# A graph attention layer on one core: 88 instead of 64 edge groups taken out of the gather

## The chip, the cores and the metric

The kernel runs on one core of a Trainium2 chip. The metric is device microseconds (us) of one execution. Engines are named as in the profile: PE (matmul), DVE (vector), ACT (scalar), POOL (GpSimd), SP (sync, which here only issues DMAs).

## The reference

One layer of graph attention, with a residual and a normalisation, over N = 12500 nodes and E = 400000 edges of 64 features each:

```python
h_src, h_dst = x[src], x[dst]
e = leaky_relu(concat([h_src, h_dst, edge]) @ W_attn + b_attn, 0.01)
m = concat([h_src, edge]) @ W_ne
alpha = softmax of e over the edges of the same dst
z = segment_sum(alpha * m, dst)
out = layernorm(x + relu(concat([x, z]) @ W_out))
```

The edges come sorted by `dst`. `dst` is drawn as 12500 u² with u uniform, so low nodes have many edges and high nodes few.

## The kernel before, in words

All work of interest is in `sorted_path` (line 53). Edges stand in 782 groups of 512: 128 partitions by T = 4 columns. The kernel treats two kinds of group differently.

**Gathered groups.** Groups 64 to 781 fetch the rows of their sources from a table in device memory. `gather` (L273) issues on POOL, for each group, four indirect DMAs of 128 rows (L280) into a tile `zx`. Four groups share a tile, and the pool holds ZB = 8 tiles. The 718 groups form 46 batches: 43 of 16 groups and, from `ENDS`, batches of 12, 12 and 6. A batch has four tiles, so the eight buffers are two batches deep: the gather of tile i of batch k+2 can begin when the products of tile i of batch k are done with its buffer. Per tile, `scores` (L305) computes the edge part of the score on DVE (L314, L316), adds the gathered part (L321, the first instruction that needs the gather), makes a one-hot of the destination (L323) and picks the destination's part (L328, L331). Per batch, `softmax` (L562) runs a segmented softmax as a chain that goes back and forth between DVE, PE and ACT: segmented scans on DVE, then L497 and L500 on PE turn a column into a line and back (`to_line`, `to_col`), and DVE waits for that at L604 and L633. Then `weights` (L669) scales the one-hots and `products` (L684, the matmuls at L689) sums weighted rows into PSUM; `add_in` (L696, L706) adds that into an SBUF ring of accumulators. Products of tiles 0 and 1 come at once, those of tiles 2 and 3 in pieces during the softmax of the next batch (`some_products`). Output blocks of 128 nodes are finished four at a time by `finish0` to `finish3` (L878 to L947) when their edges are all in.

**Dense groups.** Groups 0 to 63 belong to the lowest nodes and are not gathered. Each passes three stations:

- A *look* finds the source's part of the score: `look_products` (L376, L380) multiplies a one-hot of the source's position in its block by the scores of all 98 blocks, and `look_scores` (L383) picks the right block on DVE (L392 to L395), adds the edge's part (L389, L390) and the destination's part (L397 to L400). Two looks are done per batch, in batches 1 to 32.
- A softmax of their own, in four rounds of 16 groups, runs at batches 8, 16, 24 and 32, in the tile phase and beside the ordinary one. Such a batch is called resting here.
- A *count*: `dense_counts` (L403) builds, for each of the four columns, the position one-hot times the softmax weight (L412 on DVE) and a one-hot of block and destination slot (L410, L411 on ACT), and multiplies them (L417 on PE). `dense_sum` (L420, L426) adds the result to the tile `counts`, which thus holds the summed weight of each source node for each of ND = 16 destination slots. Two counts per batch, in batches 10 to 41. `edge_products` (L446, L452) and `edge_sum` (L460) sum the edge features of the same groups.

When a *chunk* of groups has been counted, `node_products` (L462, 13 matmuls at L467) multiplies `counts` by all of x, `node_pick` (L471) and its followers put the sums into accumulators `accd` and `acce` for nodes 0 to 127, and `counts` is cleared (L479). There are ten chunks.

Everything stands in a written-out order (`manual_schedule`): each engine executes its instructions as the Python code issues them. Inside the softmax, the generator stops at five places and calls `dense_step(n)` there, which is where dense work is put into the waits of the chain.

Of the kernel before, what the change touches and what calls it, by code (L numbers as in the profile page):

```python
# [15 lines left out]
P = 128  # L16
T = 4
# [11 lines left out]
LOWS = 1  # L29
# [5 lines left out]
DB = 4  # L35
EACH = 2
CHUNKS = ((16, 1), (8, 3), (4, 6))
NODS = (2, 3, 4, 5)
ND = 16
HC = 8  # L40
NOD = max(NODS)
# [11 lines left out]
def sorted_path(ctx, tc, x, dst, idx, edge, w_ne, w_attn, b_attn, w_out, out, flag):  # L53
# [46 lines left out]
    assert HC * ND == P and HC * D <= 512 and sum(chunk_sizes) == DG and len(NODS) == DB  # L100

    def nodes_of(g):
        return NODS[g // BS]

# [29 lines left out]
    fars = const.tile([P, NK + DB + 1], F32, name="fars")  # L134
# [4 lines left out]
    both = const.tile([P, D], F32, name="both")  # L139

# [4 lines left out]
    places = const.tile([P, NB * NOD], F32, name="places")  # L145
# [61 lines left out]
    def dense_list(d):  # L207

        srcs = pre.tile([P, BS, 2 * T], I32, name="dense_srcs", bufs=DB)
        nc.sync.dma_start(out=srcs, in_=idx[d * BS:(d + 1) * BS].rearrange("g p c -> p g c"))  # L210
        return srcs

    def dense_places(d, srcs):

        at = slice(d * BS, (d + 1) * BS)
        parted = tiny.tile([P, T, BS], I32, name="parted")
# [166 lines left out]
    def look_scores(g, j, loads, found):  # L383

        ed, wrow = loads
        many = nodes_of(g)
        pr = feats.tile([P, SG, T, D], F32, name="pr", bufs=1)
        total = tiny.tile([P, 3, T], F32, name="total")
        nc.vector.tensor_tensor(pr[:, 0], ed[:, j], w_edge.to_broadcast([P, T, D]), op=OP.mult)  # L389
        nc.vector.tensor_reduce(total[:, 0], pr[:, 0], axis=AX.X, op=OP.add)  # L390
        hits = work.tile([P, T, NB], BF16, name="hits", bufs=1)
        nc.vector.tensor_tensor(hits, count_[:, 0:NB].unsqueeze(1).to_broadcast([P, T, NB]),  # L392
                                high[:, :, g:g + 1].to_broadcast([P, T, NB]), op=OP.is_equal)
        nc.vector.tensor_tensor(found, found, hits, op=OP.mult)
        nc.vector.tensor_reduce(total[:, 1], found, axis=AX.X, op=OP.add)  # L395
        at = pr[:, 1, :, 0:many]
        nc.vector.tensor_tensor(at, slots[:, 0:many].unsqueeze(1).to_broadcast([P, T, many]),  # L397
                                slot_[:, :, g:g + 1].to_broadcast([P, T, many]), op=OP.is_equal)
        nc.vector.tensor_tensor(at, at, wrow[:, j].unsqueeze(1).to_broadcast([P, T, many]), op=OP.mult)
        nc.vector.tensor_reduce(total[:, 2], at, axis=AX.X, op=OP.add)  # L400
        nc.vector.tensor_reduce(y_dense[:, :, g % BS], total.rearrange("p c t -> p t c"), axis=AX.X, op=OP.add)

    def dense_counts(g):  # L403

        lows = work.tile([P, T, P], F32, name="lows", bufs=LOWS)
        highs = []
        wide = NB * nodes_of(g)
        for t in range(T):
# [3 lines left out]
            nc.vector.tensor_scalar(lows[:, t, :], count_, low[:, t, g:g + 1], kept[:, t, g % (2 * BS):g % (2 * BS) + 1],  # L412
# [3 lines left out]
        for t in range(T):  # L416
            nc.tensor.matmul(to, lows[:, t, :], highs[t], start=(t == 0), stop=(t == T - 1))  # L417
# [10 lines left out]
    def dense_weights(g0, n):  # L428
# [4 lines left out]
        for j in range(n):  # L433
# [12 lines left out]
    def edge_products(g0, n, ep, w, bank_):  # L446

        assert n == 2 == EACH
        many = nodes_of(g0)
        z = bank_[:, T * NB:T * NB + n * many].rearrange("p (g n) -> p g n", n=many)  # L450
        for t in range(T):
            nc.tensor.matmul(z, ep[:, t], w[:, t], start=(t == 0), stop=(t == T - 1))  # L452
        return g0, n, z

    def edge_sum(g0, n, z):

        for g in range(n):
            of = slice(g * D, (g + 1) * D)
# [103 lines left out]
    def softmax(k, about, carry, d=None):  # L562

        G = sizes[k] if d is None else BS
# [8 lines left out]
        if k and G < BS:  # L573
# [7 lines left out]
        if d is not None:  # L581
            nc.scalar.activation(yraw[:, :, 0:BS], y_dense, AF.Copy)
# [72 lines left out]
        if meets:  # L655
# [9 lines left out]
            nc.vector.memset(rtm[:, R:R + 1], FLOOR)  # L665
# [1007 lines left out]
```

## Time and profile before

| what | us |
|---|---|
| median of 3 runs (lowest, highest) | 3665.47 (3664.61, 3672.32) |
| the profiled execution, its own time | 3668.67 |
| its span, first to last instruction | 3666.9 |
| busy: POOL | 2723.0 |
| busy: PE, DVE, ACT | 2016.1, 1982.1, 943.7 |
| mean granted clock of PE | 0.667 of full speed |

The profiled execution is 1.8 us longer than its span, and 3.2 us above the median. A group of instructions is a row `line engine operation out<-in xcount | busy us, mean ns of one | idle us before them <-what ended it`. A row of the timeline is `start, duration, engine, line, operation [idle before <-releaser]`.

### The profile page before, as it was taken

The page shows a single profiled execution, that of the slowest core. Times are in us where ns is not written, and L with a number is a line of the kernel's source. Part 1 is how long each engine was busy: PE and PEld are TensorE (multiplying, and loading weights), DVE is VectorE, ACT ScalarE, POOL GpSimd, SP SyncE. Part 2 cuts the span into 40 slices and gives each one's busy share as a digit, 9 for nine tenths or more (in the row PEclk, how much of TensorE's full clock was granted, in tenths as well). Part 3 has the DMA queues.
Part 4 walks back from the last instruction along what each step waited for, and adds up shares of the span by engine and source line. Part 5 has one row for each costly group of instructions (what it writes and reads, how often), then busy time and mean ns, then how long its engine had stood idle before and what let it go on. Part 6 is the DMA issues. An engine that isn't in the chain of part 4 may idle for free.

```text
span 3666.9 us, 32998 instructions
## 1 busy us (share of the span) xinstructions
PE 2016.1 (55%) x8505; PEld 1751.5 (48%) x8505; DVE 1982.1 (54%) x5065; ACT 943.7 (26%) x2202; POOL 2723.0 (74%) x2888
## 2 busy tenths in 40 slices
PE   0144443435555544756665576566657576665754
PEld 0144443334555544655554465555545455444554
DVE  5544444444554555556555565565556565545565
ACT  1211211212222222223322233232223233222221
POOL 6777777777777777777777777777777777777772
PEclk9999999997555555655565565556656565665555
DMA  9332332223333233333333333332323233322231
GB/s 123 71 65 62 66 70 59 59 60 68 66 64 80 57 72 63 70 67 67 70 77 64 69 65 68 66 82 58 75 47 83 54 65 70 65 59 60 55 67 24
DMA packets 488960, 242.90 MB, mean 66 GB/s; under 512 B 330131, under 2 KB 442810, under 8 KB 488762
## 3 DMA queue, kind: packets, MB, share of 16 engines
q1 hardware_dynamic: 393590, 144.58, 16.9%
q0 software_dynamic: 92128, 95.80, 15.6%
q8 instruction: 70, 1.15, 0.1%
q14 instruction: 128, 1.05, 0.1%
q10 hardware_dynamic: 3044, 0.33, 0.1%
HBM read 233.74 MB, written 6.73 MB: 66 GB/s over the span
## 4 chain that ended last, share of the span: by engine, by line
POOL 38%; PE 19%; issue 16%; DVE 14%; DMA 9%; ACT 3%; DVEq 1%; SPq 0%; POOLq 0%; ACTq 0%
POOL zx L280 38%; PE pg L689 13%; DMA zx<-table,srcs 8%; PE pg L417 2%; DVE acc L706 1%; DVE hot L323 1%; DVE pr L328 1%; DVE sdst L331 1%; PE pg L380 1%; PE lines L497 1%; DVE pr L314 1%; DVE level L636 1%; DVE fixed L316 1%; PE pg L918 1%; PE lines L500 1%
## 5 line engine op out<-in xcount | busy, mean ns | idle before, releaser
L280 POOL DMA_INDIRECT zx<-table,srcs x2808 | 2652.8, 945 | 855.8 <-issue 791.8
L689 PEld LDWEIGHTS pg<-w,zx 128*128 128x128 f32 x5600 | 1212.4, 332 | 76.9 <-issue 64.7
L689 PE MATMUL pg<-w,zx 128*128 128x24 f32 (+10 forms) x5600 | 1211.4, 391 | 57.6 <-issue 55.2
L497 PE MATMUL lines<-ident,bnd 128*1 128x128 f32 x200 | 60.5, 406 | 1193.1 <-ACT bnd L594 1178.9
L497 PEld LDWEIGHTS lines<-ident,bnd 128*1 128x1 f32 x200 | 14.8, 98 | 1218.0 <-ACT bnd L594 1202.2
L321 DVE TENSOR_TENSOR fixed<-fixed,zx 128x16 f32<-128x16 f32 (+3 forms) x184 | 33.9, 184 | 701.9 <-DMA zx<-table,srcs 698.4
L314 DVE TENSOR_TENSOR pr<-ze,fixed 128x1024 f32<-128x1024 f32 (+3 forms) x184 | 219.6, 1194 | 135.8 <-ACT fixed L311 133.8
L417 PE MATMUL pg<-big,lows 128*128 128x196 f32 (+3 forms) x512 | 257.2, 672 | 15.4 <-DVE lows L412 11.1
L316 DVE TENSOR_REDUCE fixed<-pr 128x16 f32<-128x1024 f32 (+3 forms) x184 | 221.1, 1202 | 6.3
L311 ACT ACTIVATE fixed<-wrow 128x144 f32<-128x144 f32 (+10 forms) x184 | 47.7, 259 | 595.6 <-issue 239.8
L312 ACT ACTIVATE zx<-ze 128x1024 f32<-128x1024 f32 (+3 forms) x184 | 191.0, 1038 | 8.6 <-DMA zx<-table,srcs 2.1
L589 ACT ACTIVATE soft<-turned 128x128 f32<-128x128 f32 x50 | 19.3, 386 | 664.8 <-DVE turned L587 664.8
L417 PEld LDWEIGHTS pg<-big,lows 128*128 128x128 f32 x512 | 146.0, 301 | 90.5 <-issue 71.9
L706 DVE TENSOR_TENSOR acc<-acc,pg 128x16 f32 (+10 forms) x718 | 132.1, 184 | 99.3 <-PE pg L689 33.0
L410 ACT ACTIVATE big<-places,place 128x196 f32<-128x196 f32 (+3 forms) x256 | 144.9, 566 | 0.0
L380 PE MATMUL pg<-s_src,big 128*128 128x98 f32 x512 | 136.9, 446 | 0.0
L467 PE MATMUL pg<-xall,counts 128*128 128x512 f32 (+1 forms) x260 | 129.5, 659 | 0.0
L411 ACT ACTIVATE big<-big 128x196 f32<-128x196 f32 (+3 forms) x256 | 125.3, 489 | 8.1
L380 PEld LDWEIGHTS pg<-s_src,big 128*128 128x128 f32 x512 | 125.6, 330 | 0.0
L323 DVE TENSOR_TENSOR hot<-fixed,drel 128x576 bf16<-128x576 f32 (+10 forms) x184 | 113.4, 616 | 6.4
L328 DVE TENSOR_TENSOR pr<-hot,fixed 128x576 f32<-128x576 bf16 (+10 forms) x184 | 112.6, 612 | 6.3
L331 DVE TENSOR_REDUCE sdst<-pr 128x16 f32<-128x256 f32 (+12 forms) x184 | 112.5, 611 | 6.4
(289 smaller groups left out, 2272.4 us busy)
## 6 DMA issues: line engine op xcount, KB each, us to landing
ze<-in_edge_dram SPq DMA_DIRECT2D x172, 512.0 KB
zx<-table,srcs POOLq DMA_INDIRECT x2808
ed<-in_edge_dram SPq DMA_DIRECT2D x32, 256.0 KB
low_of<-low_rows SPq DMA_DIRECT2D x64, 128.0 KB
ep<-in_edge_dram SPq DMA_DIRECT2D x64, 128.0 KB
table<-xall SPq DMA_DIRECT2D x7, 455.0 KB
ze<-in_edge_dram SPq DMA_DIRECT2D x8, 384.0 KB
out_dram<-yo SPq DMA_DIRECT2D x23, 128.0 KB
```

Of the source, the lines that this page charges most:

```text
L280: nc.gpsimd.indirect_dma_start(out=zx[0:r, g, t, 1:EW] if plain else zx[0:r, g, t, 0:EW], out_offset=None, in_=x[:, :] if plain else table ...
L312: nc.scalar.activation(zx[0:r, 0:n, :, EW:EW + D], ze[0:r, 0:n], AF.Copy)
L314: nc.vector.tensor_tensor(pr[0:r, 0:n], ze[0:r, 0:n], w_edge[0:r].unsqueeze(1).to_broadcast([r, n, T, D]), op=OP.mult)
L316: nc.vector.tensor_reduce(ysum[0:r, 0:n], pr[0:r, 0:n], axis=AX.X, op=OP.add)
L323: nc.vector.tensor_tensor(hot[0:r, 0:n], slots[0:r, 0:Sk].unsqueeze(1).unsqueeze(1).to_broadcast([r, n, T, Sk]), drel[0:r, :, b:b + n].rea ...
L328: nc.vector.tensor_tensor(at[0:r, 0:n], hot[0:r, 0:n], win[0:r, 0:n, 0:Sk].unsqueeze(2).to_broadcast([r, n, T, Sk]), op=OP.mult)
L331: nc.vector.tensor_reduce(sdst[0:r, 0:n], at[0:r, 0:n], axis=AX.X, op=OP.add)
L380: nc.tensor.matmul(found[:, t, :], hot[:, :, t], s_src, start=True, stop=True)
L410: nc.scalar.activation(hi, places[:, 0:wide], AF.Square, bias=place[:, t, g:g + 1])
L417: nc.tensor.matmul(to, lows[:, t, :], highs[t], start=(t == 0), stop=(t == T - 1))
L689: nc.tensor.matmul(pg[:, g, :], zx[:, g, t, 1:EW + D], w[:, g, t, :], start=(t == 0), stop=(t == T - 1))
L706: nc.vector.tensor_tensor(ag, ag, pg[:, g, :], op=OP.add)
```

## The change

Dense groups become 88, so gathered ones 694. They pass their softmax in rounds of 24, 24, 24 and 16. Up to three looks and three counts are done per batch (`alike` stops at the end of a round, of a span with the same number of slots, and of a chunk): looks in batches 1 to 30, counts in 10 to 39. The rests stay at batches 8, 16, 24 and 32. There are 18 chunks in place of ten, and from batch 28 to 40 one in every batch. The accumulators `accd` and `acce` take nodes 0 to 255, so the first output block to be finished by this way is a pair. There are 45 batches: 41 of 16 groups, then 10, 10, 12 and 6.

The parts of three looks that don't depend on PE stand in one set of instructions (`look_rows`), placed at tile 2 of the batch; what is left of `look_scores` is four instructions, one look each in `dense_step` 0, 1 and 2. Counts start at tile 1, in step 2 and in step 3, and one `add_in` moves into step 2. `lows` has six small buffers in place of one of four columns. Several scratch tiles are shared, and `places` is 16 bits wide. In the output blocks, `x_part` multiplies two blocks of x at once by a block-diagonal weight (`twice`).

```diff
-LOWS = 1
+LOWS = 6
-DB = 4
-EACH = 2
-CHUNKS = ((16, 1), (8, 3), (4, 6))
-NODS = (2, 3, 4, 5)
+ROUNDS = (24, 24, 24, 16)
+DB = len(ROUNDS)
+EACH = 3
+CHUNKS = ((24, 1), (9, 1), (6, 2), (3, 1), (6, 1), (3, 10), (2, 2))
+NODS = ((18, 2), (36, 3), (60, 4), (88, 5))
+DBL = 2
...
-    ENDS = ((3, 3, 3, 3), (3, 3, 3, 3), (2, 2, 1, 1))
+    ENDS = ((3, 3, 2, 2), (3, 3, 2, 2), (3, 3, 3, 3), (2, 2, 1, 1))
-    DG = DB * BS
+    DG = sum(ROUNDS)
...
+    def look_rows(g0, n, loads):
+        ed, wrow = loads
+        many = nodes_of(g0)
...
+        nc.vector.tensor_tensor(pr[:, 0:n], ed[:, 0:n], w_edge.unsqueeze(1).to_broadcast([P, n, T, D]), op=OP.mult)
+        nc.vector.tensor_reduce(total[:, 0], pr[:, 0:n], axis=AX.X, op=OP.add)
...
+    def look_scores(g, found):
...
+        nc.vector.tensor_tensor(hits, hits, found, op=OP.mult)
+        picked = tiny.tile([P, T], F32, name="picked")
+        nc.vector.tensor_reduce(picked, hits, axis=AX.X, op=OP.add)
+        y = y_dense[:, :, g - begins[round_of(g)]]
+        nc.vector.tensor_tensor(y, y, picked, op=OP.add)
...
+    def x_part(c0, xtt, po, opens):
+        for j in range(0, size_of(c0), 2):
+            nc.tensor.matmul(po[:, j:j + 2, :], xtt[:, j // 2, :], twice, start=opens and j == 0, stop=False,
+                             skip_group_check=True)
...
-                    if n in (0, 3) and seen:
-                        look_scores(*seen.pop(0))
+                    if seen:
+                        look_scores(*seen.pop(0))
-                    if n == 2:
+                    if n == 0:
                         while open_counts:
                             dense_sum(*open_counts.pop(0))
+                    if n == 2 and behind:
+                        sums.append(behind.pop(0))
...
-                    if n == 1:
-                        for j, g in enumerate(batch_looks[1:]):
-                            seen.append((g, 1 + j, loads, look_products(turns.pop(0), spare())))
-                    if n == 2:
-                        for g in batch_counts[1:]:
-                            open_counts.append(dense_counts(g))
+                    if n < 2 and n + 1 < len(batch_looks):
+                        if n == 1:
+                            turns.append(look_turn(rows_ahead.pop(0)))
+                        seen.append((batch_looks[n + 1], look_products(turns.pop(0), spare())))
+                    if n > 1 and n - 1 < len(batch_counts):
+                        open_counts.append(dense_counts(batch_counts[n - 1]))
```

On POOL, the gathers of the whole program, before (`L280`) and after (`L302`); `table` is the table of rows, and the first 64 come straight from x while the table is being written:

```order
L280 DMA zx<-in_x_dram,srcs 128x64 x32
L749 DMA wk_191<-sdflat,d0p 128x48
L280 DMA zx<-in_x_dram,srcs 128x64 x32
...
L280 DMA zx<-table,srcs 128x65 x2804
L280 DMA zx<-table,srcs 32x65 x4
```

```order
L302 DMA zx<-in_x_dram,srcs 128x64 x32
L785 DMA counts<-sdflat,d0p 128x48
L302 DMA zx<-in_x_dram,srcs 128x64 x32
L785 DMA counts<-sdflat,d0p 128x48 x6
L302 DMA zx<-table,srcs 128x65 x2708
L302 DMA zx<-table,srcs 32x65 x4
```

The gathers from the table fall from 2808 to 2712, which are the four of each of 24 groups; nothing else on POOL changes its place.

On PE, the softmax of a late batch with looks and counts, before; `bnd` and `line` are the lines that the softmax turns, L380 is a look, L417 a count, L689 the products of the batch ahead:

```order
L497 MATMUL lines<-ident,bnd 1x4x32 x2
L689 MATMUL pg<-w,zx 128x32 x16
L500 MATMUL lines<-ident,line 128x1 x2
L689 MATMUL pg<-w,zx 128x32 x8
L380 MATMUL pg<-s_src,big 128x98 x4
L497 MATMUL lines<-ident,bnd 1x4x32 x2
L689 MATMUL pg<-w,zx 128x32 x8
L417 MATMUL pg<-big,lows 128x392 x4
L500 MATMUL lines<-ident,line 128x1 x2
L500 MATMUL lines<-ident,keep 128x1
```

The same place after, where L532 and L535 are the turns, L402 a look, L449 a count, L725 the products:

```order
L532 MATMUL lines<-ident,bnd 1x4x32 x2
L725 MATMUL pg<-w,zx 128x32 x16
L402 MATMUL pg<-s_src,big 128x98 x4
L535 MATMUL lines<-ident,line 128x1 x2
L725 MATMUL pg<-w,zx 128x32 x8
L402 MATMUL pg<-s_src,big 128x98 x4
L532 MATMUL lines<-ident,bnd 1x4x32 x2
L725 MATMUL pg<-w,zx 128x32 x8
L449 MATMUL pg<-big,lows 128x392 x4
L535 MATMUL lines<-ident,line 128x1 x2
L449 MATMUL pg<-big,lows 128x392 x4
L535 MATMUL lines<-ident,keep 128x1
```

A look now stands ahead of the first turn back (L535), and a second count ahead of the last one (`keep`).

On DVE, the middle of the same softmax, from the last scan ahead of the second stop to L633, before:

```order
L622 SCALAR_TENSOR_TENSOR soft<-same,soft 128x128
L422 TENSOR_LOAD rel
L426 ISA
L426 TENSOR_TENSOR counts<-counts,pg 128x98x4
L412 TENSOR_SCALAR lows<-pps,low,kept 128x128 x4
L628 SCALAR_TENSOR_TENSOR dens<-rw,lines 1x64
L630 SCALAR_TENSOR_TENSOR dens<-rw,dens,lines 1x128
L389 TENSOR_TENSOR pr<-ed,fixed 128x256
L390 TENSOR_REDUCE total<-pr 128x4
L392 TENSOR_TENSOR hits<-pps,high 128x392
...
L633 SCALAR_TENSOR_TENSOR soft<-mask,lines,soft 128x128
```

And after, where L427 to L433 are what is left of a look, L444 the one-hots of a count, and L668 stands for L633:

```order
L657 SCALAR_TENSOR_TENSOR soft<-same,soft 128x128
L427 TENSOR_TENSOR pr<-pps,high 128x392
L429 TENSOR_TENSOR pr<-pr,pg 128x392
L431 TENSOR_REDUCE picked<-pr 128x4
L433 TENSOR_TENSOR y_dense<-y_dense,picked 128x4
...
L444 TENSOR_SCALAR lows<-pps,low,kept 128x128 x4
L663 SCALAR_TENSOR_TENSOR dens<-rw,lines 1x64
L665 SCALAR_TENSOR_TENSOR dens<-rw,dens,lines 1x128
L444 TENSOR_SCALAR lows<-pps,low,kept 128x128 x4
L668 SCALAR_TENSOR_TENSOR soft<-mask,lines,soft 128x128
```

The sum of a count (L426) has left this place for an earlier one, a look and an `add_in` (left out at the dots) have come ahead of L663, and the one-hots of a third count ahead of L668.

More of the change, by code (lines that the diff above doesn't have):

```diff
@@ L99, in sorted_path, with round_of, kept_at @@
     chunk_ends = {sum(chunk_sizes[:c + 1]): n for c, n in enumerate(chunk_sizes)}
-    assert HC * ND == P and HC * D <= 512 and sum(chunk_sizes) == DG and len(NODS) == DB
+    assert HC * ND == P and HC * D <= 512 and sum(chunk_sizes) == DG == NODS[-1][0] and all(a in chunk_ends for a in begins[1:])
     def nodes_of(g):
-        return NODS[g // BS]
+        return next(n for upto, n in NODS if g < upto)
+    def round_of(g):
+        return max(d for d in range(DB) if begins[d] <= g)
+    def kept_at(g):
+        d = round_of(g)
+        return g - begins[d] + d % 2 * BD
+    edges_ = sorted({*begins, *(upto for upto, _ in NODS)})
+    spans = list(zip(edges_, edges_[1:]))
+    DN = DBL * P
     eps_col = const.tile([P, 1], F32, name="eps_col")
@@ L133, in sorted_path @@
     d0b = const.tile([P, NG], I16, name="d0b")
[L134 removed]
+    fars = const.tile([P, NK + len(spans) + 1], F32, name="fars")
     nc.vector.memset(fars, 0.0)
@@ L205, in sorted_path, with dense_list, dense_places @@
     pens = pens[0:1].rearrange("o (k i) -> o k i", k=2)
-    def dense_list(d):
-        srcs = pre.tile([P, BS, 2 * T], I32, name="dense_srcs", bufs=DB)
-        nc.sync.dma_start(out=srcs, in_=idx[d * BS:(d + 1) * BS].rearrange("g p c -> p g c"))
-        return srcs
-    def dense_places(d, srcs):
-        at = slice(d * BS, (d + 1) * BS)
-        parted = tiny.tile([P, T, BS], I32, name="parted")
+    def dense_list():
+        srcs = pre.tile([P, DG, 2 * T], I32, name="dense_srcs", bufs=1)
+        for a, b in zip(begins, begins[1:]):
+            nc.sync.dma_start(out=srcs[:, a:b], in_=idx[a:b].rearrange("g p c -> p g c"))
+        return srcs
+    def dense_places(i, srcs):
+        a, b = spans[i]
+        n = b - a
+        at = slice(a, b)
+        srcs = srcs[:, a:b]
+        parted = pre.tile([P, T, BD], I32, name="parted")[:, :, 0:n]
         ids = srcs[:, :, 0:T].rearrange("p g t -> p t g")
@@ L411, in dense_counts @@
             nc.scalar.activation(hi, hi, AF.Relu, scale=-1.0, bias=1.0)
-            nc.vector.tensor_scalar(lows[:, t, :], count_, low[:, t, g:g + 1], kept[:, t, g % (2 * BS):g % (2 * BS) + 1],
+            lows.append(work.tile([P, P], F32, name="lows", bufs=LOWS))
+            nc.vector.tensor_scalar(lows[t], count_, low[:, t, g:g + 1], kept[:, t, kept_at(g):kept_at(g) + 1],
                                     op0=OP.is_equal, op1=OP.mult)
@@ L738, in sorted_path @@
     d0p = const.tile([P, NW], I32, name="d0p")
-    wks = [const.tile([P, S], F32, name=f"wk{k}") for k in range(NW)]
+    wks = [counts.rearrange("p h n -> p (h n)")[:, k * S:(k + 1) * S] for k in range(NW)]
     nc.scalar.activation(w_dst, attn[:, D:2 * D], AF.Copy)
@@ L842, in sorted_path @@
     nc.tensor.transpose(pwt[0:D, 0, :], wne, ident)
-    wt = work.tile([D, NBC, P], F32, name="xtt", bufs=2)
+    for h in range(2):
+        nc.scalar.dma_start(out=twice[h * D:(h + 1) * D, h * D:(h + 1) * D], in_=w_out[0:D, :])
+    wt = work.tile([P, NBC // 2, P], F32, name="xtt", bufs=2)[0:D]
     nc.vector.tensor_copy(wt[:, 0, :], pwt[0:D, 0, :])
@@ L897, in front @@
     def front(c0, xtt, po, opens):
-        for j in range(min(NBC, NB - c0)):
-            nc.tensor.matmul(po[:, j, :], xtt[:, j, :], wout[:, 0, :], start=opens and j == 0, stop=False,
-                             skip_group_check=True)
+        x_part(c0, xtt, po, opens)
         return c0, po
@@ L1002, in sorted_path, with alike @@
         loads = rows_again = None
+        def alike(todo):
+            n = 0
+            while n < min(EACH, len(todo)) and not (n and todo[n] in edges_) and not (n and todo[n] in chunk_ends):
+                n += 1
+            return [todo.pop(0) for _ in range(n)]
         def drawn(steps, between_):
@@ L1100, in sorted_path @@
                     if k and i == 1 and batch_looks:
-                        seen.append((batch_looks[0], 0, loads, look_products(turns.pop(0), shared)))
+                        seen.append((batch_looks[0], look_products(turns.pop(0), shared)))
+                    if k == 1 and i == 1:
+                        nc.vector.memset(counts, 0.0)
+                    if k and i == 2 and batch_looks:
+                        look_rows(batch_looks[0], len(batch_looks), loads)
                     if k and i == 1 and batch_counts:
```

168 lines of the change are left out of this document (90 added, 78 removed).

## The prediction

> **What bounds the kernel now.** I read the page first: the chain of the work that ended last, then its group of gathers, and the DVE group that waits for them.
>
> ```profile
> span 3666.9 us, 32998 instructions
> ...
> POOL 38%; PE 19%; issue 16%; DVE 14%; DMA 9%; ACT 3%; DVEq 1%; SPq 0%; POOLq 0%; ACTq 0%
> ...
> L280 POOL DMA_INDIRECT zx<-table,srcs x2808 | 2652.8, 945 | 855.8 <-issue 791.8
> ...
> L321 DVE TENSOR_TENSOR fixed<-fixed,zx 128x16 f32<-128x16 f32 (+3 forms) x184 | 33.9, 184 | 701.9 <-DMA zx<-table,srcs 698.4
> ```
>
> POOL's gathers hold the largest share of the chain. Their idle time is nearly all "issue": POOL waits for nobody. DVE, the next candidate, waits 698 us for gathered rows. The timeline of POOL shows the rhythm near the end:
>
> ```profile
> 3299.04 0.94 POOL L280 DMA_INDIRECT zx<-table,srcs  x1 [0.30 <-issue]
> 3300.29 0.94 POOL L280 DMA_INDIRECT zx<-table,srcs  x1 [0.30 <-issue]
> ```
>
> One gather every 1.25 us. A batch of 16 groups has 64, so 80 us. The windows view (stretch, its length, then busy us of PE, PE loads, DVE, ACT, POOL with counts, clock, DMA share, GB/s) compares an early stretch, with no dense work, and a late one, with all of it:
>
> ```profile
> 375.00:450.00 75.00, 28.46 (x133) 27.38 (x133) 28.81 (x84) 10.04 (x26) 56.70 (x61) 1.00 0.30 63
> 2100.00:2175.00 75.00, 59.52 (x228) 47.19 (x228) 50.08 (x126) 29.23 (x71) 56.72 (x61) 0.62 0.34 73
> ```
>
> DVE's work nearly doubles, PE's doubles at a lower granted clock, and POOL issues the same 61 gathers. So the body is bound by the number of gathers, as long as each batch gets its other work done within 80 us. What is left of those 80 us is DVE's wait at the last tile of a batch:
>
> ```profile
> 2581.97 0.18 DVE L321 TENSOR_TENSOR fixed<-fixed,zx 128x16 f32<-128x16 f32 x1 [8.86 <-DMA zx<-table,srcs]
> 2661.84 0.18 DVE L321 TENSOR_TENSOR fixed<-fixed,zx 128x16 f32<-128x16 f32 x1 [11.21 <-DMA zx<-table,srcs]
> ```
>
> These two are late batches with two looks and two counts: 79.9 us apart, with 9 to 11 us to spare.
>
> **Part 1: fewer gathers.** 24 groups by 4 gathers are 96 gathers fewer, at 1.25 us: 120.0 us less on POOL. The order shows the 96 gone from one uninterrupted row. Alone this would give 3668.7 − 120.0 = 3548.7 us in the profiled execution.
>
> **Part 2: a third look and a third count per batch.** Prices per group are the busy time of a row over its 64 groups:
>
> ```profile
> L389 DVE TENSOR_TENSOR pr<-ed,fixed 128x256 f32<-128x256 f32 x64 | 25.0, 391 | 0.0
> L390 DVE TENSOR_REDUCE total<-pr 128x4 f32<-128x256 f32 x64 | 26.9, 420 | 2.2
> L392 DVE TENSOR_TENSOR hits<-pps,high 128x392 bf16<-128x392 f32 x64 | 35.5, 555 | 0.0
> L394 DVE TENSOR_TENSOR pg<-pg,hits 128x392 f32<-128x392 f32 x64 | 36.8, 574 | 3.9
> L395 DVE TENSOR_REDUCE total<-pg 128x4 f32<-128x392 f32 x64 | 36.2, 566 | 2.2
> L412 DVE TENSOR_SCALAR lows<-pps,low,kept 128x128 f32<-128x128 f32 x256 | 87.0, 401 | 0.0
> L426 DVE TENSOR_TENSOR counts<-counts,pg 128x196 f32 (+3 forms) x64 | 33.4, 522 | 14.8 <-issue 11.8
> ```
>
> ```profile
> L380 PE MATMUL pg<-s_src,big 128*128 128x98 f32 x512 | 136.9, 446 | 0.0
> L417 PE MATMUL pg<-big,lows 128*128 128x196 f32 (+3 forms) x512 | 257.2, 672 | 15.4 <-DVE lows L412 11.1 <-ACT big L411 3.6 <-ACT big L410 0.7
> L467 PE MATMUL pg<-xall,counts 128*128 128x512 f32 (+1 forms) x260 | 129.5, 659 | 0.0
> ```
>
> On DVE a look's five large instructions take 2.5 us; a third adds at most that, since the small ones are now shared. A count is 1.4 us of one-hots (87.0/64) and 0.5 of sum. With an estimated 1 us for the third group's edge weights and sums (five or six small instructions like L321's 0.18 us), DVE gets 5.4 us more per batch. On PE a look is 2.1 us (136.9/64), a count 4.0, a chunk 13.0 (129.5/10).
>
> What PE gets matters only where DVE waits for it, in the softmax:
>
> ```profile
> 2594.78 0.36 DVE L604 SCALAR_TENSOR_TENSOR soft<-pen,lines,soft 128x128 f32<-128x128 f32 x1 [2.94 <-PE lines L500]
> 2608.65 0.36 DVE L633 SCALAR_TENSOR_TENSOR soft<-mask,lines,soft 128x128 f32<-128x128 f32 x1 [4.21 <-PE lines L500]
> ```
>
> The first wait gets a look ahead of it (+2.1 us), the second between nothing and a count (0 to 4.0). Against that, a look's four instructions (1.7 us from the three large rows L392 to L395) now stand inside the first wait, and one-hots inside the second. So the added length of a batch lies between 3 (DVE's 5.4 less what hides in the waits) and 12 us (5.4 + 2.1 + 4.0, nothing hidden). I take 6, near DVE's own sum, because the waits already have room for about as much as PE adds. All of it is covered by the 9 to 11 us of spare. At 12 the tightest batches would run 3 us over, and the next part says what absorbs that. The 13 us of a chunk now come in every batch from 28 to 40, but at its end, when PE is ahead of DVE. Their pick and sums on DVE stood in every second late batch before; I bound them by the 2.3 us by which the spare of the two neighbours above differs, and the tighter one of them is the one I count with.
>
> **Part 3: rests, rounds and the depth of the buffers.** At the resting batch 32 DVE's last tile was not waited for:
>
> ```profile
> 2760.58 0.18 DVE L321 TENSOR_TENSOR fixed<-fixed,zx 128x16 f32<-128x16 f32 x1
> ...
> 2767.26 6.88 PE L689 MATMUL pg<-w,zx 128*128 128x36 f32 x32
> ...
> 2780.43 0.94 POOL L280 DMA_INDIRECT zx<-table,srcs  x1 [0.30 <-ACT big L411]
> ```
>
> It came 98.7 us after its predecessor at 2661.84, so 18.7 late. The products of tile 2 end at 2774.1, and the gather into that buffer starts at 2780.43: 6.3 us of slack still. A batch may thus be about 25 us late before POOL feels it. The rests stay at the same batches, the one at 32 now has no looks beside it (two looks gone, −5 us on DVE) but one count more and a round of the same 16, so I leave its lateness as it is. The rounds of 24 fall at 8, 16 and 24, where fewer slots per group make every other step shorter. Cost 0; if the cover is gone, each us beyond costs one us of POOL, which I bound at 10 us for the four rests together.
>
> **Part 4: the front.** The dense lists come in one tile, and their preparation has seven spans in place of four:
>
> ```profile
> 75.62 0.22 DVE L218 TENSOR_SCALAR parted<-dense_srcs 128x64 int32<-128x64 int32 x1 [23.79 <-DMA dense_srcs<-in_idx_dram]
> ```
>
> DVE idles 23.8 us there already; a list longer by 24 of 64 groups (at most 24/64 of that wait, 8.9 us), and three more spans of six or so instructions like this one's 0.22 us, make batch 0 some 5 to 13 us later. That is under the 25 us that buffers take. Cost 0.
>
> **Part 5: the end.** Rows of the last tile of batches 40, 42, 43, 44 and 45, and the finishes of a four-block and a one-block piece:
>
> ```profile
> 3301.74 0.18 DVE L321 TENSOR_TENSOR fixed<-fixed,zx 128x16 f32<-128x16 f32 x1 [10.21 <-DMA zx<-table,srcs]
> ...
> 3461.69 0.18 DVE L321 TENSOR_TENSOR fixed<-fixed,zx 128x16 f32<-128x16 f32 x1 [14.03 <-DMA zx<-table,srcs]
> ...
> 3504.66 0.42 DVE L934 SCALAR_TENSOR_TENSOR pg<-pg,xall 128x256 f32<-128x256 f32 x1
> ...
> 3508.28 0.42 DVE L947 TENSOR_TENSOR yo<-pg,var 128x256 f32<-128x256 f32 x1
> ...
> 3521.68 0.18 DVE L321 TENSOR_TENSOR fixed<-fixed,zx 128x12 f32<-128x12 f32 x1 [2.61 <-DMA zx<-table,srcs]
> ...
> 3524.35 0.22 DVE L934 SCALAR_TENSOR_TENSOR pg<-pg,xall 128x64 f32<-128x64 f32 x1
> ...
> 3527.25 0.22 DVE L947 TENSOR_TENSOR yo<-pg,var 128x64 f32<-128x64 f32 x1
> ...
> 3582.32 0.18 DVE L321 TENSOR_TENSOR fixed<-fixed,zx 128x12 f32<-128x12 f32 x1 [1.27 <-DMA zx<-table,srcs]
> ...
> 3629.18 0.16 DVE L321 TENSOR_TENSOR fixed<-fixed,zx 32x4 f32<-32x4 f32 x1
> ```
>
> Less its wait, DVE's time from one to the next is 57.4 us (to batch 43), 59.4 (44) and 46.9 (45); gathers need 60, 60 and 30. So the very end is DVE's: 16.9 us late at the last tile, and 37.7 more to the end of the span. A four-block finish is 4.0 us, a one-block finish 3.1, and a group 1.6 us ((59.4 − 3.1 − 46.9)/6). After, batch 40's last gather comes at the same time as before, since all batches to 40 gather the same number. Then: ten groups, 57.4 − 3.1 = 54.3 against 50.0, 4.3 late; ten groups with the pair's finish but no four-block one, 59.4 − 3.1 − 4.0 = 52.3 against 50.0, 6.6 late; twelve groups without the small finish, 56.3 against 60, 2.9 late; six groups as before. The end comes 2.9 us later against the gathers than it did. Bounds: −4 (`x_part` halves some matmuls) to +13 (all of a chunk's 13.0 us on PE in the way of a short batch).
>
> **Sum.** 3668.7 − 120.0 + 2.9 = 3551.6 us beside the profiled execution; less the 3.2 that this lay above the median, 3548.4.
>
> **Rivals.**
>
> *The dense batches overrun a little (0.13).* Lateness adds up to the rest at batch 32, and POOL waits for a buffer a few times: speaking for it are the 6.3 us of slack there. 10 to 40 us of the gain go: 3558 to 3588.
>
> *The dense batches overrun for good: slower (0.04).* Place: batches 10 to 39, at POOL's wait for a buffer of tile 2. To lose 120 us and the 25 that buffers absorb, 30 batches must each run 145/30 = 4.8 us over 80, so the third group must cost at least 9 + 4.8 = 14 us per batch. At 16 us it is (16 − 9) × 30 − 25 = 185 us lost, and 3731 us. My upper bound is 12, so this needs PE's granted clock, 0.62 there, to fall further and every matmul with it.
>
> *Gathers slow down with DVE's work (0.03).* DVE's one-hots L412 grow by 24 × 1.36 = 33 us. If POOL could not issue beside them, it would lose that: 3581 us. The trace speaks against it:
>
> ```profile
> 2597.73 1.35 DVE L412 TENSOR_SCALAR lows<-pps,low,kept 128x128 f32<-128x128 f32 x4
> ...
> 2598.00 0.95 POOL L280 DMA_INDIRECT zx<-table,srcs  x1 [0.30 <-issue]
> 2599.26 0.94 POOL L280 DMA_INDIRECT zx<-table,srcs  x1 [0.30 <-issue]
> ```
>
> The gather beside them has its usual 0.95 us, and the next starts 1.26 us later. The Trainium skill, page "SBUF — State Buffer", section "Who interferes with whom", states that GpSimd and some DVE instructions, `tensor_scalar` in its two-port modes among them, exclude each other from a shared pair of SBUF ports. By that rule the gathers would stretch wherever such instructions run; this trace shows no stretch.
>
> *Nothing comes of it (0.02).* The end of the kernel could follow something other than the number of gathers. The 61 gathers in either window, and L280's "issue" idle time, speak against it. 3665 us.
>
> **Chances.** Forecast with its own bounds, 3541 to 3558: 0.78. Range: it reaches into the first rival, to 3577; below, to 3541, for an end 4 us better and some us of noise in the runs. Faster by over 0.2% (7 us, about what these measurements can tell): the forecast, the first and the third rival, 0.94; same 0.02; slower 0.04.
>
> **What would show it.** POOL's row with 2712 gathers of about 945 ns and no idle time but "issue"; the last gather 120 us earlier; L321's successor still ending waits of 2 to 8 us in batches 28 to 39; last tiles of the last four batches 4, 7, 3 and 20 us behind their gathers. Wrong would be POOL idle behind the products of tile 2 or 3, or batches over 80 us apart.

## The result and the profile after

| | before | after |
|---|---|---|
| median of the runs on the first chip (lowest, highest), us | 3665.68 (3664.61, 3672.32) | 3542.84 (3541.20, 3544.34) |
| the profiled execution, its own time | 3668.67 | 3541.20 |
| its span | 3666.9 | 3539.4 |

The ratio is 0.9661, with a 95% interval of 0.9644 to 0.9678: 122.8 us less. The forecast was 3548.4 us, in a range of 3541 to 3577, so the result lies near the lower end.

The page of the changed kernel: the span, the gathers, and the DVE group that waits for them.

```profile
span 3539.4 us, 34643 instructions
...
L302 POOL DMA_INDIRECT zx<-table,srcs x2712 | 2558.7, 943 | 826.7 <-issue 769.9
...
L343 DVE TENSOR_TENSOR fixed<-fixed,zx 128x16 f32<-128x16 f32 (+2 forms) x180 | 33.1, 184 | 556.4 <-DMA zx<-table,srcs 552.7
```

There are 96 gathers fewer, each as long as before (943 against 945 ns), and POOL's idle time is still "issue". DVE's wait for gathered rows fell from 698 to 553 us, over 45 batches in place of 46: most of the third looks and counts went there. The windows view of the changed kernel for the late stretch that the prediction showed (stretch, length, busy PE, PE loads, DVE, ACT, POOL, clock, DMA, GB/s):

```profile
2100.00:2175.00 75.00, 54.05 (x216) 40.69 (x215) 55.70 (x140) 31.43 (x70) 56.61 (x60) 0.63 0.41 83
```

DVE is at 55.7 of 75 us, against 50.1 before, and POOL issues as ever. Now the timeline of a late batch with three looks and three counts: DVE at the last tile of batch 28, at its two waits for PE in the softmax, and at the last tile of batch 29.

```profile
2340.13 0.18 DVE L343 TENSOR_TENSOR fixed<-fixed,zx 128x16 f32<-128x16 f32 x1 [7.30 <-DMA zx<-table,srcs]
...
2356.84 0.36 DVE L639 SCALAR_TENSOR_TENSOR soft<-pen,lines,soft 128x128 f32<-128x128 f32 x1
...
2368.80 0.36 DVE L668 SCALAR_TENSOR_TENSOR soft<-mask,lines,soft 128x128 f32<-128x128 f32 x1 [1.19 <-PE lines L535]
...
2419.98 0.18 DVE L343 TENSOR_TENSOR fixed<-fixed,zx 128x16 f32<-128x16 f32 x1 [7.88 <-DMA zx<-table,srcs]
```

The late batch before, shown in the prediction, had waits of 2.94 and 4.21 us in its softmax where now none and 1.19 stand, and 8.86 and 11.21 us of spare where now 7.30 and 7.88 are left. The added work filled most of the waits and took some 1 to 4 us of the spare.

The softmax of a rest starts behind the resting batch's own softmax and runs in the tile phase of the next batch, so the rests at 24 and 32 show at the last tiles of batches 25 (L343 at 2114) and 33. Here are these, and the gather that needs the buffer behind the latter:

```profile
2114.09 0.18 DVE L343 TENSOR_TENSOR fixed<-fixed,zx 128x16 f32<-128x16 f32 x1
...
2757.68 0.18 DVE L343 TENSOR_TENSOR fixed<-fixed,zx 128x16 f32<-128x16 f32 x1
...
2778.09 0.94 POOL L302 DMA_INDIRECT zx<-table,srcs  x1 [0.30 <-ACT big L441]
```

DVE came to both tiles late and waited for neither, but POOL's gap is its usual 0.30 us. Last, the end: POOL's last gather of the kernel before, then of the changed kernel, and DVE at the last tile of its last five batches, at its wait for PE (L668) ahead of the fourth of these, and at its last instruction.

```profile
3608.72 0.86 POOL L280 DMA_INDIRECT zx<-table,srcs  x1 [0.30 <-issue]
```

```profile
3299.13 0.18 DVE L343 TENSOR_TENSOR fixed<-fixed,zx 128x16 f32<-128x16 f32 x1 [14.03 <-DMA zx<-table,srcs]
...
3352.79 0.17 DVE L343 TENSOR_TENSOR fixed<-fixed,zx 128x8 f32<-128x8 f32 x1
...
3404.22 0.17 DVE L343 TENSOR_TENSOR fixed<-fixed,zx 128x8 f32<-128x8 f32 x1
...
3421.65 0.36 DVE L668 SCALAR_TENSOR_TENSOR soft<-mask,lines,soft 128x128 f32<-128x128 f32 x1 [1.28 <-PE lines L535]
...
3458.72 0.18 DVE L343 TENSOR_TENSOR fixed<-fixed,zx 128x12 f32<-128x12 f32 x1 [3.87 <-DMA zx<-table,srcs]
...
3485.80 0.87 POOL L302 DMA_INDIRECT zx<-table,srcs  x1 [0.30 <-issue]
...
3504.19 0.16 DVE L343 TENSOR_TENSOR fixed<-fixed,zx 32x4 f32<-32x4 f32 x1
...
3533.14 0.29 DVE L992 TENSOR_TENSOR yo<-pps,var 128x128 f32<-128x128 f32 x1
```

Between the two profiled executions the span fell by 127.5 us. The last gather starts 122.9 us earlier (3608.72 to 3485.80). From there to DVE's last tile it was 20.5 us (3629.18) and is 18.4: 2.1 less. From there to the end of the span it was 37.7 and is 35.2: 2.5 less. The three add up to the 127.5.

### The profile page after: what moved, and what is told of

It is laid out like the page before. It is cut to its first block, busy times and chain, and to the rows that moved or that the text cites. A ratio compares the mean times of both kernels' runs of the same rounds, so it can differ in the third digit from the quotient of the medians.

```text
span 3539.4 us, 34643 instructions
## 1 busy us (share of the span) xinstructions
PE 2088.3 (59%) x9022; PEld 1745.4 (49%) x9022; DVE 2063.0 (58%) x5197; ACT 1071.7 (30%) x2449; POOL 2628.4 (74%) x2792
## 5 line engine op out<-in xcount | busy, mean ns | idle before, releaser
L302 POOL DMA_INDIRECT zx<-table,srcs x2712 | 2558.7, 943 | 826.7 <-issue 769.9
L725 PEld LDWEIGHTS pg<-w,zx 128*128 128x128 f32 x5408 | 1127.0, 321 | 57.1 <-DVE w L711 42.1
L725 PE MATMUL pg<-w,zx 128*128 128x20 f32 (+9 forms) x5408 | 1128.7, 382 | 38.1 <-DVE w L711 34.5
L532 PE MATMUL lines<-ident,bnd 128*1 128x128 f32 x196 | 59.1, 405 | 1100.8 <-ACT bnd L629 1079.6
L532 PEld LDWEIGHTS lines<-ident,bnd 128*1 128x1 f32 x196 | 13.9, 97 | 1124.6 <-ACT bnd L629 1101.4
L343 DVE TENSOR_TENSOR fixed<-fixed,zx 128x16 f32<-128x16 f32 (+2 forms) x180 | 33.1, 184 | 556.4 <-DMA zx<-table,srcs 552.7
L449 PE MATMUL pg<-big,lows 128*128 128x490 f32 (+3 forms) x704 | 323.2, 619 | 4.6 <-DVE lows L444 4.6
L336 DVE TENSOR_TENSOR pr<-ze,fixed 128x1024 f32<-128x1024 f32 (+2 forms) x180 | 212.4, 1180 | 154.4 <-ACT fixed L333 154.4
L501 PE MATMUL pg<-xall,counts 128*128 128x512 f32 (+1 forms) x468 | 237.0, 668 | 37.7 <-DVE earlies L1168 34.4
L333 ACT ACTIVATE fixed<-wrow 128x80 f32<-128x80 f32 (+9 forms) x180 | 46.9, 261 | 593.4 <-issue 251.1
L449 PEld LDWEIGHTS pg<-big,lows 128*128 128x128 f32 x704 | 175.6, 265 | 100.3 <-issue 61.5
L338 DVE TENSOR_REDUCE fixed<-pr 128x16 f32<-128x1024 f32 (+2 forms) x180 | 214.1, 1189 | 6.2
L441 ACT ACTIVATE big<-places,place 128x490 f32<-128x490 int16 (+3 forms) x352 | 204.9, 582 | 0.0
L402 PE MATMUL pg<-s_src,big 128*128 128x98 f32 x704 | 189.7, 449 | 0.0
L334 ACT ACTIVATE zx<-ze 128x1024 f32<-128x1024 f32 (+2 forms) x180 | 185.2, 1029 | 8.3 <-issue 0.9
L442 ACT ACTIVATE big<-big 128x490 f32<-128x490 f32 (+3 forms) x352 | 178.1, 506 | 11.2
L402 PEld LDWEIGHTS pg<-s_src,big 128*128 128x128 f32 x704 | 172.4, 329 | 0.6
L742 DVE TENSOR_TENSOR acc<-acc,pg 128x16 f32 (+9 forms) x694 | 128.4, 185 | 69.8 <-issue 19.9
L444 DVE TENSOR_SCALAR lows<-pps,low,kept 128x128 f32<-128x128 f32 x352 | 122.3, 399 | 46.1 <-PE pg L449 45.5
```

What stands on the lines that cost most here:

```text
L302: nc.gpsimd.indirect_dma_start(out=zx[0:r, g, t, 1:EW] if plain else zx[0:r, g, t, 0:EW], out_offset=None, in_=x[:, :] if plain else table ...
L334: nc.scalar.activation(zx[0:r, 0:n, :, EW:EW + D], ze[0:r, 0:n], AF.Copy)
L336: nc.vector.tensor_tensor(pr[0:r, 0:n], ze[0:r, 0:n], w_edge[0:r].unsqueeze(1).to_broadcast([r, n, T, D]), op=OP.mult)
L338: nc.vector.tensor_reduce(ysum[0:r, 0:n], pr[0:r, 0:n], axis=AX.X, op=OP.add)
L402: nc.tensor.matmul(found[:, t, :], hot[:, :, t], s_src, start=True, stop=True)
L441: nc.scalar.activation(hi, places[:, 0:wide], AF.Square, bias=place[:, t, g:g + 1])
```

## The experiments

The theory: time is the number of gathers by 1.25 us, plus an end on DVE; dense work is free as long as a batch's lateness stays within what the buffers absorb. The main rival: DVE's or PE's work in the dense batches, or the re-ordering of the softmax, already decides a good part. To put numbers on the theory I took from the trace each batch's own DVE time, from last tile to last tile without the waits for gathers. I chained these with 1.25 us per gather, and let POOL wait where the products behind a buffer are late.

The first four ran side by side on a second chip, on which the kernel before took 3671.54 us.

**The changed kernel again.**

> The changed kernel unaltered, beside the next three on the same chip. Either theory: about 3543 us.

Measured: 3548.74 us, ratio 0.9664 (0.9651 to 0.9677). The ratio is that of the first chip; both kernels are 6 us longer here. The last section says where that lies.

**The code without the fewer gathers** (`code_64`).

```diff
-ROUNDS = (24, 24, 24, 16)
+ROUNDS = (16, 16, 16, 16)
-EACH = 3
+EACH = 2
-CHUNKS = ((24, 1), (9, 1), (6, 2), (3, 1), (6, 1), (3, 10), (2, 2))
+CHUNKS = ((16, 1), (8, 3), (4, 6))
-NODS = ((18, 2), (36, 3), (60, 4), (88, 5))
+NODS = ((16, 2), (32, 3), (48, 4), (64, 5))
-    ENDS = ((3, 3, 2, 2), (3, 3, 2, 2), (3, 3, 3, 3), (2, 2, 1, 1))
+    ENDS = ((3, 3, 3, 3), (3, 3, 3, 3), (2, 2, 1, 1))
```

> The changed code with the numbers of before: 64 dense groups in rounds of 16, two looks and two counts per batch, chunks and end batches as before, so 2872 gathers again. Theory (time is gathers times 1.25 us plus an end on DVE): the gain goes with the 96 gathers, 3655 to 3667 us. Rival (the re-ordered softmax, the shared look rows and the paired x part bring a good part of the gain): 3600 us or so. A look at DVE's wait for the last tile of batches 10 to 40 also says what the re-ordering alone is worth per batch: I expect 1 to 3 us more spare than in the kernel before.

Measured: 3668.10 us, ratio 0.9991 (0.9982 to 1.0000), 3.4 us less than the kernel before beside it. So the gain goes with the gathers; the changed kernel beside it is 119.4 us faster, and the rival's 3600 us is far off. The median of 3668 lies just above the top of what I expected, as both kernels are some 6 us longer on this chip. Its profile has the group of waits and, at the end, DVE's wait for PE ahead of batch 44's last tile, and the last tiles of batches 44 and 45:

```profile
L343 DVE TENSOR_TENSOR fixed<-fixed,zx 128x16 f32<-128x16 f32 (+3 forms) x184 | 33.9, 184 | 719.7 <-DMA zx<-table,srcs 716.3
...
3549.52 0.36 DVE L668 SCALAR_TENSOR_TENSOR soft<-mask,lines,soft 128x128 f32<-128x128 f32 x1 [3.03 <-PE lines L535]
...
3585.43 0.18 DVE L343 TENSOR_TENSOR fixed<-fixed,zx 128x12 f32<-128x12 f32 x1 [1.24 <-DMA zx<-table,srcs]
...
3630.37 0.16 DVE L343 TENSOR_TENSOR fixed<-fixed,zx 32x4 f32<-32x4 f32 x1
```

The waits are 716 us against 698 over all tiles, of which some 4 come from gathers that were 1.4 ns further apart in this profile. DVE's own time, from last tile to last tile without these waits, is 10 us less in all: up to 4 us less in some batches, up to 3 us more in others. At the last tiles of batches 10 to 40, where I had expected 1 to 3 us more spare each, the wait is 313 us in place of 332, so the spare there did not grow. The last batch takes 44.9 us of DVE in place of 46.9, with the same six groups.

**One matmul per block for the x part** (`x_single`).

```diff
-        for j in range(0, size_of(c0), 2):
-            nc.tensor.matmul(po[:, j:j + 2, :], xtt[:, j // 2, :], twice, start=opens and j == 0, stop=False,
-                             skip_group_check=True)
+        for j in range(size_of(c0)):
+            nc.tensor.matmul(po[:, j, :], xtt[:, j // 2, :], twice[:, j % 2 * D:(j % 2 + 1) * D], start=opens and j == 0,
+                             stop=False, skip_group_check=True)
```

> The changed kernel with one matmul per block for the x part again in place of one per pair (26 more pairs of columns on PE, some 0.4 us per batch, and nothing at the very end). Theory: PE is not waited for there, so within 2 us of the changed kernel, 3541 to 3545 us. Rival (PE's time in the output blocks lies on the path at the end): 3 to 8 us slower.

Measured: 3548.92 us, 0.2 us from the changed kernel beside it. The paired x part brings nothing that can be measured. (The absolute band was written for the first chip.)

**More work on DVE in the dense batches** (`pad_8`).

```diff
+                if batch_counts:
+                    for _ in range(9):
+                        pr = feats.tile([P, SG, T, D], F32, name="pr", bufs=1)
+                        nc.vector.memset(pr, 0.0)
                 for i, (g0, n, zx, hot) in enumerate(parts):
                     w = weights(g0, n, hot, b0)
```

> The changed kernel with nine memsets of 128x1024 more on DVE, some 8 us, between the softmax and the weights of each of the 30 batches that have counts. Theory (8 to 12 us of spare per batch, and two batches of buffers that swallow some 25 us of lateness): nearly free; chaining the measured batches, each with 8 us more, gives 9 us of POOL waiting for a buffer at batch 32, so 3543 to 3558 us. Rival (DVE's work in the dense batches is already on the path): up to 30 x 8 = 240 us, 3780 us.

Measured: 3595.08 us, 46.3 more than the changed kernel beside it: neither the 9 us expected nor the rival's 240. The added group and POOL's longest wait say why.

```profile
L1273 DVE MEMSET pr<- 128x1024 f32 x270 | 246.2, 912 | 72.0 <-DVE pr L1273 67.1 <-issue 4.9
...
2819.18 0.95 POOL L302 DMA_INDIRECT zx<-table,srcs  x1 [29.91 <-issue]
```

The row also has 72.0 us of idle time ahead of the memsets, nearly all put down to the memset before: (246.2 + 72.0)/30 is 10.6 us per batch, and not 8. Chaining the batches with 10.6 us more gives 45.3 us, against 46.3 measured, and most of it in one place: POOL waits 29.9 us for a buffer after the rest at batch 32. The mechanism held, and my price of the padding was wrong. That the price accounts for it was worked out after the run.

The next four ran on another chip, beside runs of the kernel before at 3664.66 us; they are compared with the first 3542.84.

**Twice the padding** (`pad_16`: eighteen memsets).

> As the kernel with nine memsets more per batch with counts, but eighteen, some 16 us. Theory: now past the spare in nearly every one of the 30 batches; chaining the measured batches gives about 178 us more, 3690 to 3740 us, slower than the kernel before. This is the point from which the slower rival of the prediction decides. If dense work were hidden without limit: 3543 us; if it were all on the path: 3543 + 480 = 4020 us.

Measured: 3870.96 us, ratio to the kernel before 1.0565 (1.0534 to 1.0596): slower by 206 us, and 328 above the changed kernel, where 178 were expected.

```profile
L1273 DVE MEMSET pr<- 128x1024 f32 x540 | 492.5, 912 | 147.5 <-DVE pr L1273 142.6 <-issue 4.9
...
L302 POOL DMA_INDIRECT zx<-table,srcs x2712 | 2558.7, 943 | 1152.3 <-issue 1059.8 <-ACT fixed L333 29.1 <-DMA zx<-table,srcs 22.9
```

The padding is (492.5 + 147.5)/30 = 21.3 us per batch; the chain then gives 323 us. With the price mended, theory and measurement are 5 us apart. POOL's gathers are not slower, 943 ns each, but its idle time has grown from 827 to 1152 us. So the slower rival of the prediction is a real mechanism, and by the chain it costs the whole gain at an estimated 14 us more per batch than the changed kernel has now (13.5 gives 115 us, 14 gives 128). That point was not run.

**More gathers** (`more_gathers`).

```diff
         zx = feats.tile([P, SG, T, EW + D], F32, name="zx")
+        if not plain and g0 + n < NG:
+            spare_rows = tiny.tile([P, EW], F32, name="spare_rows", bufs=3)
+            nc.gpsimd.indirect_dma_start(
+                out=spare_rows, out_offset=None, in_=table[:, :],
+                in_offset=bass.IndirectOffsetOnAxis(ap=srcs[:, g0 - b0, 0:1], axis=0))
```

> The changed kernel with one gather more per tile from batch 1 on, of 128 rows into a scratch tile that nobody reads: 175 gathers more. Theory (POOL's issue is the bound): 175 x 1.25 = 219 us, 3757 to 3764 us. Rival (the end follows DVE or PE in good part): clearly less, under 3700 us.

Measured: 3788.23 us, 245.4 more, above the expected 219 and outside the band.

```profile
L300 POOL DMA_INDIRECT spare_rows<-table,srcs x175 | 165.1, 943 | 80.4 <-issue 38.6 <-PE pg L730 17.2 <-DMA spare_rows<-table,srcs 10.0
...
764.42 0.94 POOL L300 DMA_INDIRECT spare_rows<-table,srcs  x1 [2.78 <-DMA spare_rows<-table,srcs]
```

165.1 us of work and 80.4 of idle time ahead of it make 245.5, which is what the kernel got longer. The usual gap would be 53 us of the idle time (175 by 0.30); without the other 27 the added gathers cost 1.25 us each. The excess is most likely my scratch tile: POOL issues most of the added gathers four in a row, there are three buffers, and all of the excess stands in fifteen longer waits, the last of a row as in the second line. The profile names a landing there, at others it names PE or DVE.

**Fewer gathers, with the dense work as it is** (`fewer_gathers`).

```diff
             for t in range(T):
+                if not plain and g == t == 0 and g0 + n < NG:
+                    nc.sync.dma_start(out=zx[:, 0, 0, 0:EW], in_=table[0:P, :])
+                    continue
                 r = RP if g0 + g == NG - 1 else P
```

> The changed kernel with one of the 16 gathers of each tile from batch 1 on replaced by a plain DMA of the first 128 rows of the table, issued by SP: that part of the result is then of other rows. 175 gathers fewer, 75 us per batch of 16. Theory: nearly all of 219 us goes, less what the resting batches then lack in cover: 3335 to 3350 us. Rival (DVE has little left): the body stays at 80 us per batch in the dense part and no more than 100 us go, 3440 us.

Measured: 3344.68 us, 198.2 less, within the band. The groups of gathers and of DVE's waits:

```profile
L305 POOL DMA_INDIRECT zx<-table,srcs x2537 | 2393.5, 943 | 785.3 <-issue 723.1 <-DMA zx<-table,srcs 18.3 <-PE pg L728 13.1
...
L346 DVE TENSOR_TENSOR fixed<-fixed,zx 128x16 f32<-128x16 f32 (+2 forms) x180 | 33.1, 184 | 359.7 <-DMA zx<-table,srcs 348.0 <-DMA zx<-table 7.4
```

The 175 gathers are worth 1.13 us each, so nearly the full 1.25 even at 75 us per batch, and DVE still waits 348 us for gathered rows. So over most of the run the rest of the work is not yet the bound at 75 us per batch; behind the rests at 24 and 32 it is, where five and three last tiles in a row come without a wait.

**Seven buffers** (`buffers_7`).

```diff
-ZB = 8
+ZB = 7
```

> The changed kernel with seven buffers for gathered tiles in place of eight, so 20 us less of cover behind every tile. Theory (late batches are swallowed by the depth of the buffers, smallest cover 6.7 us behind batch 32 and 11.5 behind batch 24): POOL now waits some 13 us after batch 32, 8 after batch 24, some more in the short batches at the end; 3563 to 3577 us. Rival (the cover is never used): no change, 3543 us.

Measured: 3569.36 us, 26.5 more, in the band. POOL's waits for the buffers behind batches 24 and 32:

```profile
2125.30 0.94 POOL L302 DMA_INDIRECT zx<-table,srcs  x1 [8.33 <-ACT line L539]
...
2778.77 0.94 POOL L302 DMA_INDIRECT zx<-table,srcs  x1 [14.67 <-issue]
```

8.3 and 14.7 us stand against 8 and 13 expected. With eight buffers these rests cost nothing, and only just: one buffer is 20 us, so by these waits, less the usual 0.30, an estimated 12 us of cover are left behind batch 24 and 5.6 behind batch 32.

**96 dense groups** (`groups_96`), with the changed kernel beside it:

```diff
-ROUNDS = (24, 24, 24, 16)
+ROUNDS = (24, 24, 24, 24)
-CHUNKS = ((24, 1), (9, 1), (6, 2), (3, 1), (6, 1), (3, 10), (2, 2))
+CHUNKS = ((24, 1), (9, 1), (6, 2), (3, 1), (6, 1), (3, 14))
-NODS = ((18, 2), (36, 3), (60, 4), (88, 5))
+NODS = ((18, 2), (36, 3), (60, 4), (96, 5))
-    ENDS = ((3, 3, 2, 2), (3, 3, 2, 2), (3, 3, 3, 3), (2, 2, 1, 1))
+    ENDS = ((3, 3, 3, 3), (3, 3, 3, 3), (3, 3, 2, 2), (2, 2, 1, 1), (2, 2, 1, 1))
```

> The changed kernel unaltered, beside the kernel with 96 dense groups on the same chip. Either theory: 3541 to 3549 us, by the chip.

> The changed kernel with 96 dense groups: four rounds of 24, looks in batches 1 to 32, counts to 41, and 40 batches of 16 followed by 12, 12, 10, 6 and 6. 32 gathers fewer, 40 us less on POOL. If gathers alone set the time: 3503 us. Theory (the dense work now reaches into the short batches at the end, where DVE needs 64, 64, 54, 45 and 45 us against 60, 60, 50, 30 and 30 of gathers, so its last tile is 42 us behind the last gather in place of 15, and the rest at batch 32, again with looks beside it, makes POOL wait some 3 to 8 us): 5 to 12 us less than the changed kernel on the same chip. Rival (the dense work has no room left): slower than the changed kernel.

Measured: 3534.88 us (3532.27 to 3537.31), ratio to the kernel before 0.9624 (0.9611 to 0.9637); the changed kernel beside it 3548.87 (3541.52 to 3549.73). That is 14 us less, a little more than the 5 to 12 expected, and faster than both kernels; but 26 of the 40 us that the 32 gathers are worth were given back. POOL's wait behind the rest at 24, DVE at the last tiles of the last five batches, and POOL's first wait there:

```profile
2146.47 0.94 POOL L302 DMA_INDIRECT zx<-table,srcs  x1 [4.68 <-issue]
...
3294.34 0.18 DVE L343 TENSOR_TENSOR fixed<-fixed,zx 128x12 f32<-128x12 f32 x1
...
3358.90 0.18 DVE L343 TENSOR_TENSOR fixed<-fixed,zx 128x12 f32<-128x12 f32 x1
...
3413.79 0.17 DVE L343 TENSOR_TENSOR fixed<-fixed,zx 128x8 f32<-128x8 f32 x1
3424.83 0.95 POOL L302 DMA_INDIRECT zx<-table,srcs  x1 [7.64 <-issue]
...
3453.29 0.17 DVE L343 TENSOR_TENSOR fixed<-fixed,zx 128x4 f32<-128x4 f32 x1
...
3500.21 0.16 DVE L343 TENSOR_TENSOR fixed<-fixed,zx 32x4 f32<-32x4 f32 x1
```

None of these tiles is waited for: DVE is behind from batch 40 on (64.6, 54.9, 39.5 and 46.9 us for gathers of 60, 50, 30 and 30), until POOL itself waits for buffers. POOL's waits come to 23 us, 4.4 of them behind the rest at 24 and none behind that at 32, where I had expected 3 to 8. In return the last tile is 25.9 us behind the last gather, 7.6 more than in the changed kernel, and not 27 more as expected. Two things changed at the end: counts now reach into the batches of 12 (64.6 us, where the kernel before takes 57.4 for such a batch without counts), and there are two batches of six groups in place of one (39.5 and 46.9 us against 30 of gathers). The run does not separate them.

## Why the prediction came out as it did

- **Part 1, the gathers**: right. 120.0 us was the whole of the gain in the forecast, and the last gather came 122.9 us earlier. `code_64` shows that it goes with the number of gathers; `fewer_gathers` that one is worth 1.13 us when it goes, and `more_gathers` 1.25 us when it is added, the waits at the scratch tile left out.
- **Part 2, a third look and count**: the direction was right, the size too large. I took 6 us, between 3 and 12. DVE's own time in looks-only batches rose from 47.7 to 51 to 52 us, in early batches with counts by about 4. The step that missed is "the waits already have room for about as much as PE adds": they had more. In `code_64`, with the same order and two of each, DVE waits 4.6 us at L668 in batches 11 to 15; in the changed kernel it waits 0.9 to 1.2 us there, so that some 3.5 us of the third group fit in. DVE still waits 7.3 to 11.8 us at the last tiles of batches 28 to 39, other than 33 and 34 behind the rest, where I had forecast 2 to 8. It cost nothing in the sum, as all of it was hidden.
- **Part 3, rests and buffers**: the covering was right, the reasoning at batches 8, 16 and 24 was not. With a round of 24, and a third look and count beside it, the rest at 24 put the last tile behind it 16.4 us after the last gather, where it was 5.8 before; I had taken every other step to be shorter there. The buffers took it, and `buffers_7` shows by what margin.
- **Part 4, the front**: right, no cost: DVE's last tile of batch 1 comes at 182.9 us, 182.7 before. The 5 to 13 us by which batch 0 was to be later did not come either: its last tile is at 118.0, 117.8 before.
- **Part 5, the end**: wrong in sign. Of the 10.4 us by which the profiled pair beat the sum (127.5 in place of 117.1), 5.0 are here: I expected the last tile 2.9 us later against the gathers, and it came 2.1 earlier. The four steps of 54.3, 52.3, 56.3 and 46.9 us were measured at 53.7, 51.4, 50.6 and 45.5. The 56.3 failed most. I had taken 3.1 us off for the small finish of block 0; in `code_64`, in the same code, the twelve groups that have it take 59.0 us, 8.4 more than the 50.6 here without it. Set row by row against that stretch of `code_64`, the rows of the finish (L979 to L992) are 3.5 us of the 8.4, close to the 3.1. The other 4.9 I had not taken off: the stretch also holds the softmax and sums of the batch before, which has ten groups here and twelve there. They are spread over many rows; the largest piece is DVE's wait for PE at L668, 1.28 us in place of 3.03. And the moved `add_in` was not in my sum at all; the re-ordering as a whole shortens the last batch from 46.9 to 44.9 us in `code_64`, with the same groups as before. Another 2.9 us are the earlier gathers beyond 120.0, and 2.5 lie behind the last tile; most of these two is told in the last section. On the medians 5.6 us are missing in place of 10.4. That the changed kernel took 3548.74 us on the second chip, nearly the forecast, is a coincidence: the kernel before was 6 us longer there too.
- **The rivals**: a small overrun and a lasting one both need some 8 us or more on top of a batch (by the chain, 8 us lose about 10), and the padding shows them in full: 46 us lost at 10.6, 328 at 21.3. Gathers stretching beside DVE's one-hots: the one-hots grew from 87.0 to 122 us, and the 71 gathers that ran beside them for over 0.7 us took 944 ns on average, those with no one-hot beside them 943. That the Trainium skill ("SBUF — State Buffer", "Who interferes with whom") has GpSimd and some DVE instructions exclude each other did not show in these gathers; which of these instructions run in a two-port mode, no run tells.

## What to carry to other kernels

Where one engine issues without a wait, count its instructions first: removing n of them is worth n times its period, until another engine's time per stage reaches the same length. Work added elsewhere is priced by each stage's spare and by how many stages of lateness the buffers swallow, and the resting stages and the short ones at the end use that up first. Chaining measured stage times gave the cost of the padding to within 5 us once the padding itself was measured; with an assumed price it had missed by 37 and 150 us. A piece of padding has to be measured before it is used as a ruler.

## What the runs showed of the hardware

A kernel's executions differ by about 0.2%, on one chip too: the changed kernel beside `groups_96` ran once at 3541.52 and four times at 3548.6 to 3549.7. In the profiles the mean gather takes 943, 945 or 946 ns: 943 in the changed kernel's first profile, 945 in that of the kernel before, 946 in the changed kernel's second. The last gather and the last tile of the changed kernel in its second profile:

```profile
3491.09 0.87 POOL L302 DMA_INDIRECT zx<-table,srcs  x1 [0.30 <-issue]
...
3509.37 0.16 DVE L343 TENSOR_TENSOR fixed<-fixed,zx 32x4 f32<-32x4 f32 x1
```

The last gather is 5.3 us later than the 3485.80 of the first profile, with the same instructions: 2 ns more for each of 2776 gathers. The other 1.8 us lie behind the last tile (37.0 us to the end in place of 35.2). Windows over that stretch, first and second profile, show PE's granted clock (third figure from the end) at 0.55 and at 0.50, and the last twelve matmuls took 279 ns each in the first and 425 in the second:

```profile
3504.00:3539.00 35.00, 13.86 (x213) 12.16 (x213) 18.44 (x66) 5.77 (x15) 0.00 (x0) 0.55 0.04 9
```

```profile
3509.00:3546.00 37.00, 16.02 (x213) 14.20 (x213) 18.63 (x66) 5.86 (x16) 0.00 (x0) 0.50 0.04 8
```

```profile
L952 PE MATMUL pps<-both,acc 128*128 128x64 f32 x12 | 1.6, 279 | 0.7 <-DVE acc L742 0.7
```

```profile
L952 PE MATMUL pps<-both,acc 128*128 128x64 f32 x12 | 2.8, 425 | 0.3 <-DVE acc L742 0.3
```

The kernel before has 0.50 there too, and 37.7 us. The two do not go together: `x_single` has gathers of 946 ns and 35.4 us behind the last tile. What sets the rhythm of the gathers, or the clock at the end, stays open. A difference below 0.3% is safe only where the gathers have the same rhythm in both profiles.
